# Score rows by VectorE's square transposes, and mask fills by ScalarE, in a four-layer graph attention kernel

## The chip, the cores and the metric

The kernel runs on one core of a Trainium2 chip. The metric is the device time of one launch in microseconds (us). A profile of one execution stands beside it; times inside it are read from that execution.

## The reference

128 small graphs of 128 nodes with 512 features each pass through four graph-attention layers. In every layer the features are normalised and rectified, the layer is applied, and its output is added to its input:

```python
for layer in (L0, L1, L2, L3):
    h = maximum(layernorm(x), 0)
    x = x + layer(h, adj)
```

Layer 1 has four heads of 256 columns and then a second attention with one head. Layer 3 has eight heads of 64 columns:

```python
# layer 1, first part (softmax over the source axis, per head)
xl = (x @ W1).reshape(B, N, H, F)
asrc, adst = einsum(xl, att_src), einsum(xl, att_dst)
e = leaky_relu(asrc[:, :, None, :] + adst[:, None, :, :], 0.2)
attn = softmax(where(mask, e, -1e9), axis=1)
# layer 3
xh = (x @ W_proj) by heads
scores = leaky_relu(a_src[..., None] + a_dst[..., None, :] + b_att, 0.2)
att = softmax(where(A > 0, scores, -1e30), axis=-1)
out = relu(att @ xh)
```

All arithmetic is in float32. A score is the sum of one number per row node and one number per column node. The number of the row node is a column of 128 values over the partitions, which an engine can add as a per-partition bias. The number of the column node is needed as a row of 128 values that is the same on every partition. Making such rows is what this case is about.

## The kernel before, in words

A graph is a generator (`graph`, with `layer0` to `layer3`) that yields one instruction, or a group of instructions, at a time. Ten graphs are in flight (`FLYING = 10`). A planner (`Scheduler`) merges their instructions into one program order ahead of time: at each step it issues the instruction that could start earliest by its own cost figures (`Step.estimate`), and the older graph where two are equal. The order on each engine is therefore fixed, and an engine that waits for one instruction holds up all that stand behind it. A stream that needs a buffer takes it (`Take`) from a named set of fixed size and stops until one is given back. PSUM has eight banks, all taken under the name `bank`.

The steps that the change touches:

- **Rows through HBM.** `rows_in_dram` takes some columns (4 for layer 1's `fx`, 16 for layer 3's `f`, 8 for layer 3's `mx`). TensorE transposes them against `ident` into a bank, ScalarE copies the bank to the tile `r`, one transfer on SyncE's queue (SP) writes `r` to a small HBM buffer `d`, and `d` is then read back with every partition receiving all of it.
- **Layer 1.** A second SP transfer spreads `d` over the score tile `e` (`e<-d`, 256 KB). VectorE then adds the mask and takes the maximum of each head.
- **Layer 3.** The tile `sd` holds the scores of eight heads in two arrangements, `d` and `e`, each 128x1024. First each half is filled with eight copies of a 128x128 mask (`m3`, and its transpose `m3t`) by an SP transfer of 512 KB from SBUF to SBUF. Then the rows of `f` are added to the whole of `sd` by an accumulating transfer that GpSimd (POOL) issues (`sd<-d`, 1024 KB). VectorE takes the maxima of `d`; they become `mx`, go through `rows_in_dram` again, and a second accumulating transfer (512 KB) subtracts them in `e`. ScalarE applies its Prelu head by head and one exponential, and TensorE multiplies (`x,sd`).
- **The last five graphs** (`LATE = 5`) build layer 3's rows on TensorE and VectorE instead (`add_rows`), without HBM.

Of the kernel before, what the change touches and what calls it, by code (L numbers as in the profile page):

```python
# [19 lines left out]
SLOPE = 0.2  # L20
EPS = 1e-5
FLYING = 10
AHEAD = 2
LATE = 5
# [18 lines left out]
class Step:  # L43
# [17 lines left out]
    def estimate(self, name, outs, ins, kw):  # L61

        if name == "dma_start":

            rate, busy = (290e3, 0.35) if self.engine == "SP" else (105e3, 1.0)
            self.moves = size(outs[0]) * outs[0].shape[0] * 4 / rate
            return busy, 1.0
        n = max(size(a) for a in outs[:1] + ins)
        if self.engine == "PE":
            if name == "transpose":  # L70
                return 0.109, 0.2
            return 2 * max(0.00084 * size(outs[0]), 0.108), 0.2
        if self.engine == "DVE":
            if name == "bn_stats":
                return 0.6, 0.12
            if name == "bn_aggr":
                return 0.09, 0.12
            per = 1 / 960
            if name == "tensor_scalar" and n >= 256:
                per /= 2  # L80
            return n * per + 0.07, 0.12
        if self.engine == "ACT":
            pointers = sum(isinstance(kw.get(k), bass.AP) for k in ("bias", "scale"))
            busy = n * 0.00081 + 0.105 + (0, 0.075, 0.135)[pointers]
            return busy + 0.1 * ("accum_out" in kw), 0.15
        if self.engine == "POOL":
            if kw.get("op") == ALU.pow or ALU.pow in kw.get("ops", ()):
                return 0.6, 0.1
            return (0.25 if n <= 16 else 0.55 if name == "tensor_scalar" else 1.3), 0.1
        raise ValueError(name)  # L90


class Group(Step):
    def __init__(self, steps):
        self.engine = steps[0].engine
        self.calls = [c for s in steps for c in s.calls]
# [3 lines left out]
        self.delay = steps[-1].delay  # L100


# [33 lines left out]
class Scheduler:  # L136
# [100 lines left out]
    def issue(self):  # L237
# [17 lines left out]
        if step.moves:  # L255

            self.moved = max(end, self.moved) + step.moves
            end = self.moved + 1.0
        for name in step.writes:
# [20 lines left out]
def kernel(  # L280
# [30 lines left out]
    K3 = l3_watt.shape[1] // 2  # L311
    AG = 4 if B % 4 == 0 else 1


# [128 lines left out]
    def fold(blocks, vecs, per, to):  # L443
# [4 lines left out]
        for g in range(0, len(blocks), 4):  # L448
            wt = yield from transposed(blocks[g : g + 4], "ht", 3)
            yield Group(  # L450
                [
                    T.matmul(
                        pf[:, j // per * k : (j // per + 1) * k],
                        lhsT=wt[:, j - g, :],
                        rhs=vecs[:, j, :],
                        start=(j % per == 0),
                        stop=(j % per == per - 1),
                    )
                    for j in range(g, g + 4)
                ]  # L460
            )
            give_back(wt)
        n = len(blocks) // per * k
# [32 lines left out]
    def norm_relu(xt):  # L496

        st6 = column("st6", nc.vector.BN_STATS_DIM)
        yield V.bn_stats(st6, xt)
        mv = column("mv", nc.vector.BN_AGGR_DIM)  # L500
        yield V.bn_aggr(mv, st6)
        ve = column("ve")
        yield G.tensor_scalar(ve, mv[:, 1:2], EPS, None, ALU.add)
        rstd = column("rstd")
        yield G.tensor_tensor(out=rstd, in0=ve, in1=minus_half, op=ALU.pow)
        nmr = column("nmr")
        yield V.scalar_tensor_tensor(nmr, mv[:, 0:1], -1.0, rstd, ALU.mult, ALU.mult)
        h = yield tile_of("h", 4, D)
        yield A.activation(out=h, in_=xt, func=AF.Relu, bias=nmr, scale=rstd)
        return h  # L510

# [17 lines left out]
    def transposed(blocks, tag, bufs):  # L529

        n = len(blocks)
        r = yield tile_of(tag, bufs, n, P)
# [4 lines left out]
        yield A.copy(r.rearrange("p m q -> p (m q)"), pt[:, : n * P])  # L537
        give_back(pt)
        return r

    def rows_in_dram(cols, n):

        r = yield Take(work, [2 * H3, P], "r", 4)
        r = r[:n]
        pt = yield bank()
        yield T.transpose(pt[:n, :P], cols, ident)
        yield A.copy(r, pt[:n, :P])
        give_back(pt)
        d = dram.tile([n, P], F32, tag=f"d{n}", name="d")
        yield S.dma_start(out=d, in_=r)  # L550
        give_back(r)
        return d.rearrange("n q -> (n q)").partition_broadcast(P)

    def spread(cols, n, to):

        d = yield from rows_in_dram(cols, n)
        yield S.dma_start(out=to, in_=d)

# [18 lines left out]
    def added(cols, to, late, rows=None):  # L577

        if late:
            yield from add_rows(cols, to)  # L580
            return
        if rows is None:
            rows = yield from rows_in_dram(cols, cols.shape[1])
        yield G.dma_start(out=to, in_=rows, accum_op=ALU.add)

    def attention(own, rows, e, mask, nh, exact=False):

        mx = column(f"mx{nh}", nh)  # L590
        yield Group(
            [
                V.tensor_tensor_reduce(
                    out=e[:, j, :],
                    in0=rows[j],
# [9 lines left out]
        )  # L605
        if rows[0].tensor.name != e.tensor.name:
            give_back(rows[0])
# [6 lines left out]
        if exact:  # L614
            ef = e.rearrange("p h q -> p (h q)")
            yield V.tensor_scalar(ef, ef, own, None, ALU.add)
            yield V.scalar_tensor_tensor(ef, ef, SLOPE, ef, ALU.mult, ALU.max)
        else:
            for j in range(nh):
                yield A.activation(  # L620
                    out=e[:, j, :],
                    in_=e[:, j, :],
                    func=AF.Prelu,
# [3 lines left out]
        for j in range(nh):  # L627
            yield A.activation(
                out=e[:, j, :],
                in_=e[:, j, :],  # L630
                func=AF.Exp,
# [7 lines left out]
    def attended(own, other, mask, values, exact=False):  # L639

        e = yield tile_of("e0", 3, 1, P)
        pb = yield bank()
        yield T.transpose(pb[:, :P], other.to_broadcast([P, P]), ident)
        rz = yield from attention(own, [pb[:, :P]], e, mask, 1, exact)
        et = yield from transposed([e[:, 0, :]], "et0", 3)
        give_back(e)
        pa = yield bank()
        yield T.matmul(pa, lhsT=et[:, 0, :], rhs=values, start=True, stop=True)
        give_back(et)
        return pa, rz  # L650

    def projected(lhs, n_k, w, parts, to, beside=None, plus=None):
# [4 lines left out]
        for i in range(parts):  # L657
            lo = i * width
            pm = yield bank()
            for g in range(0, n_k, 4):  # L660
# [3 lines left out]
                            pm[:, :width],  # L664
                            lhsT=lhs[:, c, :],
                            rhs=w[c][:, lo : lo + width],
# [40 lines left out]
    def layer1(xt, mask):  # L707
# [4 lines left out]
        fx = yield tile_of("xl", 2, E1 + HF)  # L712
        e = yield tile_of("e1", 3, H1, P)
        rows = e.rearrange("p h q -> p (h q)")
        fork = yield from projected(
            ht, KC, w1x, 3, columns(fx, 3), lambda: spread(fx[:, :H1], H1, rows)
        )
        give_back(ht)
        xl = fx[:, E1:]
        yield Join(fork)  # L720
        rz = yield from attention(fx[:, H1:E1], [e[:, j, :] for j in range(H1)], e, mask, H1)
        yield V.tensor_tensor(e, e, rz.unsqueeze(2).to_broadcast([P, H1, P]), ALU.mult)
        et = yield from transposed([e[:, j, :] for j in range(H1)], "et1", 3)
        give_back(e)
        y = yield tile_of("y1", 2, FC, P)
        for g in range(0, FC, 4):
# [5 lines left out]
                        lhsT=xl[:, c * P : (c + 1) * P],  # L732
                        rhs=et[:, c * P // F1, :],
                        start=True,
# [11 lines left out]
            give_back(po)  # L746
        give_back(fx, et)
        yf = y.rearrange("p c q -> p (c q)")
# [8 lines left out]

        yield from projected(y, FC, w2x, 2, columns(gx, 2), plus=columns(b2, 2))
        give_back(y)
# [17 lines left out]
    def layer3(xt, mask, mask_t, late):  # L777
# [22 lines left out]
        )  # L800
        give_back(ht)
        f = small.tile([P, 2, H3], F32, tag="f3", name="f3")
# [72 lines left out]
    def graph(b):  # L875
# [91 lines left out]
```

## Time and profile before

| | |
|---|---|
| median of 3 runs | 3410.86 us (3410.47 to 3410.93) |
| profiled execution, its own time | 3414.4 us |
| span of its trace | 3412.6 us |
| TensorE matmul busy | 3381.6 us, 99% of the span |
| VectorE busy | 2617.3 us, 77% |
| ScalarE busy | 2316.5 us, 68% |
| GpSimd busy | 871.6 us, 26% |
| moved by DMA | 450.33 MB, mean 132 GB/s |

The busy time of TensorE counts each matmul from its start to a modelled end, and neighbours overlap; what one costs in a full stream is the distance from its start to the next start. PE is TensorE's matmuls, PEld its weight loads, DVE VectorE, ACT ScalarE, POOL GpSimd, and SPq the queue on which SyncE issues transfers. Nearly all instructions have one line number, because the planner issues them; the names of the tiles tell them apart.

### The profile page before, as it was taken

The page shows a single profiled execution, that of the slowest core. Times are in us where ns is not written, and L with a number is a line of the kernel's source. Part 1 is how long each engine was busy: PE and PEld are TensorE (multiplying, and loading weights), DVE is VectorE, ACT ScalarE, POOL GpSimd, SP SyncE. Part 2 cuts the span into 40 slices and gives each one's busy share as a digit, 9 for nine tenths or more (in the row PEclk, how much of TensorE's full clock was granted, in tenths as well). Part 3 has the DMA queues.
Part 4 walks back from the last instruction along what each step waited for, and adds up shares of the span by engine and source line. Part 5 has one row for each costly group of instructions (what it writes and reads, how often), then busy time and mean ns, then how long its engine had stood idle before and what let it go on. Part 6 is the DMA issues. An engine that isn't in the chain of part 4 may idle for free.

```text
span 3412.6 us, 56516 instructions
## 1 busy us (share of the span) xinstructions
PE 3381.6 (99%) x17118; PEld 2650.2 (78%) x17118; DVE 2617.3 (77%) x9296; ACT 2316.5 (68%) x6661; POOL 871.6 (26%) x1791
## 2 busy tenths in 40 slices
PE   8999999999999999999999999999999999999998
PEld 5777777777777777777777777777777777777787
DVE  6777777777778777777777787777787777777766
ACT  4667676677677667666767766776776676667764
POOL 1222322222222222222222222222222222222221
PEclk7999999999999999999999999999999999999998
DMA  5155555555556556555655555565565555556553
GB/s 151 45 125 127 139 139 132 131 142 138 131 126 151 129 132 145 132 128 140 143 130 132 133 144 133 138 142 128 123 151 134 134 138 135 131 131 143 131 126 97
DMA packets 392879, 450.33 MB, mean 132 GB/s; under 512 B 27128, under 2 KB 309120, under 8 KB 376832
## 3 DMA queue, kind: packets, MB, share of 16 engines
q0 software_dynamic: 35424, 193.48, 29.3%
q1 hardware_dynamic: 352976, 253.23, 25.4%
q8 instruction: 137, 2.24, 0.3%
q14 instruction: 166, 1.36, 0.1%
q10 hardware_dynamic: 4176, 0.02, 0.1%
HBM read 277.11 MB, written 35.33 MB: 92 GB/s over the span
## 4 chain that ended last, share of the span: by engine, by line
PE 98%; ACT 1%; DVE 1%; issue 0%; DMA 0%; POOL 0%; ACTq 0%; POOLq 0%; DVEq 0%
PE bank L252 98%; DVE sd L252 0%; ACT ht L252 0%; DMA a<-in_L_gnn_a_dram 0%; ACT h L252 0%; ACT sd L252 0%; ACT e L252 0%; DMA at<-in_adj_dram 0%; POOL rstd L252 0%; DVE st L252 0%; DVE products L252 0%; DVE xt L252 0%; DVE e L252 0%; POOL ve L252 0%; DVE mx L252 0%
## 5 line engine op out<-in xcount | busy, mean ns | idle before, releaser
L252 PE MATMUL bank<-w2x,y 128*128 128x257 f32 x4096 | 975.2, 381 | 0.0
L252 PE MATMUL bank<-w1x,ht 128*128 128x344 f32 x3072 | 954.3, 454 | 1.4 <-ACT ht L252 1.4
L252 PEld LDWEIGHTS bank<-w2x,y 128*128 128x128 f32 x4096 | 746.8, 190 | 108.3 <-issue 16.7
L252 PEld LDWEIGHTS bank<-w1x,ht 128*128 128x128 f32 x3072 | 572.2, 191 | 261.1 <-issue 17.9
L252 ACT ACTIVATE h<-xt,nmr,rstd 128x512 f32<-128x512 f32 x512 | 413.6, 808 | 386.1 <-DVE nmr L252 385.0
L252 PE MATMUL bank<-wpx,ht 128*128 128x264 f32 x2048 | 501.9, 388 | 0.0
L252 POOL TENSOR_SCALAR ve<-mv 128x1 f32<-128x1 f32 x512 | 173.5, 339 | 1095.1 <-DVE mv L252 905.5
L252 PEld LDWEIGHTS bank<-wpx,ht 128*128 128x128 f32 x2048 | 381.1, 191 | 87.4 <-DVE y L252 8.6
L252 ACT ACTIVATE sd<-sd,f 128x128 f32<-128x128 f32 x1024 | 366.2, 392 | 0.0
L252 ACT ACTIVATE e<-e,nm 128x128 f32<-128x128 f32 x896 | 351.4, 396 | 13.8 <-DVE e L252 9.5
L252 DVE BATCH_NORM_STATS2 st<-xt 128x6 f32<-128x512 f32 x512 | 350.7, 685 | 0.0
L252 POOL TENSOR_TENSOR rstd<-ve,minus_half 128x1 f32<-128x1 f32 x512 | 313.7, 613 | 42.0
L252 PEld LDWEIGHTS bank<-x,sd 128*128 128x128 f32 x2048 | 266.1, 194 | 48.2 <-issue 12.2
L252 POOL DMA_DIRECT2D sd<-d x246 | 230.7, 994 | 267.5 <-ACT sd L252 136.7
L252 PEld LDWEIGHTS bank<-et,xl 128*128 128x128 f32 x2048 | 250.3, 192 | 38.4 <-issue 37.5
L252 PE MATMUL bank<-et,xl 128*128 128x128 f32 x2048 | 271.8, 276 | 0.2 <-ACT et L252 0.2
L252 PE MATMUL bank<-x,sd 128*128 128x65 f32 x2048 | 260.1, 271 | 7.2 <-ACT sd L252 7.2
L252 PE MATMUL bank<-h,et 128*128 128x512 f32 x512 | 266.1, 601 | 0.7 <-ACT et L252 0.7
L252 ACT COPY xl<-bank 128x344 f32<-128x344 f32 x384 | 166.7, 434 | 135.0 <-PE bank L252 134.6
L252 DVE TENSOR_TENSOR y<-bank,b 128x512 f32<-128x512 f32 x256 | 176.8, 690 | 81.4 <-PE bank L252 72.9
L252 ACT COPY x<-bank 128x264 f32<-128x264 f32 x256 | 96.0, 375 | 210.1 <-PE bank L252 209.9
L252 DVE SCALAR_TENSOR_TENSOR xt<-bank,rz,xt 128x512 f32<-128x512 f32 x256 | 191.3, 747 | 23.6 <-PE bank L252 23.5
(90 smaller groups left out, 5207.0 us busy)
## 6 DMA issues: line engine op xcount, KB each, us to landing
sd<-d POOLq DMA_DIRECT2D x123, 1024.0 KB, 11.0
sd<-m SPq DMA_DIRECT2D x128, 512.0 KB
sd<-m3t SPq DMA_DIRECT2D x128, 512.0 KB
sd<-d POOLq DMA_DIRECT2D x123, 512.0 KB, 8.3
xt<-in_x_dram SPq DMA_DIRECT2D x128, 256.0 KB
e<-d SPq DMA_DIRECT2D x128, 256.0 KB
out_dram<-xt SPq DMA_DIRECT2D x128, 256.0 KB
at<-in_adj_dram SPq DMA_DIRECT2D x32, 256.0 KB
```

What stands on the lines that cost most here:

```text
L252: method(*args, **kw)
```

## The change

`rows_in_dram` no longer uses TensorE, a bank or ScalarE. VectorE transposes 128x32 columns in squares of 32x32, so that a row of 128 values comes out as four pieces of 32 on four groups of partitions, and four SP transfers write the pieces to `d`. Where there are fewer than 32 columns they are repeated to fill the square (layer 3), or the next columns of the same tile come along unused (layer 1). Layer 3's two mask fills become two ScalarE copies of 128x1024. Besides, the planner's cost figures for transfers are other ones, one graph instead of two is loaded ahead, five small tiles of the normalisation become one (`st`, six buffers), and some buffer sets change: `r` 4 to 5 (of another shape), `et1` 3 to 2, `m1` 10 to 7.

```diff
-AHEAD = 2
+AHEAD = 1
@@ estimate
-            rate, busy = (290e3, 0.35) if self.engine == "SP" else (105e3, 1.0)
-            self.moves = size(outs[0]) * outs[0].shape[0] * 4 / rate
-            return busy, 1.0
+            moved = size(outs[0]) * outs[0].shape[0] * 4
+            if self.engine == "POOL":
+                self.moves = moved / 165e3
+                return 1.0, 3
+            run = 4 * min(a.shape[-1] for a in outs + ins)
+            self.moves = moved / (280e3 if run > 512 else 220e3)
+            return (0.5 if max(len(a.shape) for a in outs + ins) > 2 else 0.35), 1.5
@@ issue
-            end = self.moved + 1.0
+            end = self.moved + 0.3
@@ tile_four_gat_layers_kernel
+    Q = nc.vector.STREAM_SQUARE_SIZE
+    R = P // Q
@@
-    def rows_in_dram(cols, n):
-        r = yield Take(work, [2 * H3, P], "r", 4)
-        r = r[:n]
-        pt = yield bank()
-        yield T.transpose(pt[:n, :P], cols, ident)
-        yield A.copy(r, pt[:n, :P])
-        give_back(pt)
-        d = dram.tile([n, P], F32, tag=f"d{n}", name="d")
-        yield S.dma_start(out=d, in_=r)
+    def rows_in_dram(cols, n, heads_inside=False):
+        r = yield tile_of("r", 5, Q)
+        yield V.transpose(r, cols)
+        d = dram.tile([R, n, Q] if heads_inside else [n, R, Q], F32, tag=f"d{n}", name="d")
+        yield Group(
+            [
+                S.dma_start(
+                    out=d[c] if heads_inside else d[:, c], in_=r[c * Q : c * Q + n]
+                )
+                for c in range(R)
+            ]
+        )
         give_back(r)
-        return d.rearrange("n q -> (n q)").partition_broadcast(P)
+        return d.rearrange("n c b -> (n c b)").partition_broadcast(P)
+
+    def repeated(cols):
+        n = cols.shape[1]
+        return cols.unsqueeze(1).to_broadcast([P, Q // n, n])
@@ added
-            rows = yield from rows_in_dram(cols, cols.shape[1])
+            rows = yield from rows_in_dram(repeated(cols), cols.shape[1])
@@ layer1
-        fork = yield from projected(
-            ht, KC, w1x, 3, columns(fx, 3), lambda: spread(fx[:, :H1], H1, rows)
-        )
+        def rows():
+            d = yield from rows_in_dram(fx[:, :Q], H1)
+            yield S.dma_start(out=e, in_=d)
+        fork = yield from projected(ht, KC, w1x, 3, columns(fx, 3), rows)
...
-        et = yield from transposed([e[:, j, :] for j in range(H1)], "et1", 3)
+        et = yield from transposed(heads, "et1", 2)
@@ layer3
         for to, m in (d, mask), (e, mask_t):
-            yield S.dma_start(out=to, in_=m.unsqueeze(1).to_broadcast([P, H3, P]))
+            yield A.copy(to, m.unsqueeze(1).to_broadcast([P, H3, P]))
             give_back(m)
...
-        fork = None if late else (yield Fork(rows_in_dram(mx, H3)))
+        fork = None if late else (yield Fork(rows_in_dram(repeated(mx), H3)))
@@ graph
-        m1 = yield tile_of("m1", FLYING, P)
+        m1 = yield tile_of("m1", 7, P)
```

More of the change, by code (lines that the diff above doesn't have):

```diff
@@ L100, in __init__ @@
         self.delay = steps[-1].delay
+        self.moves = sum(s.moves for s in steps)
 class Take:
@@ L453, in fold @@
                         pf[:, j // per * k : (j // per + 1) * k],
-                        lhsT=wt[:, j - g, :],
+                        lhsT=wt[j - g],
                         rhs=vecs[:, j, :],
@@ L461, in fold @@
             )
-            give_back(wt)
+            give_back(wt[0])
         n = len(blocks) // per * k
@@ L496, in norm_relu @@
     def norm_relu(xt):
[L498 to L504, printed above, removed]
+        n = nc.vector.BN_STATS_DIM
+        st = yield tile_of("st", 6, n + 5)
+        yield V.bn_stats(st[:, :n], xt)
+        mean, var = st[:, n : n + 1], st[:, n + 1 : n + 2]
+        yield V.bn_aggr(st[:, n : n + 2], st[:, :n])
+        ve, rstd, nmr = (st[:, i : i + 1] for i in range(n + 2, n + 5))
+        yield G.tensor_scalar(ve, var, EPS, None, ALU.add)
         yield G.tensor_tensor(out=rstd, in0=ve, in1=minus_half, op=ALU.pow)
-        nmr = column("nmr")
-        yield V.scalar_tensor_tensor(nmr, mv[:, 0:1], -1.0, rstd, ALU.mult, ALU.mult)
+        yield V.scalar_tensor_tensor(nmr, mean, -1.0, rstd, ALU.mult, ALU.mult)
         h = yield tile_of("h", 4, D)
         yield A.activation(out=h, in_=xt, func=AF.Relu, bias=nmr, scale=rstd)
+        give_back(st)
         return h
@@ L531, in transposed @@
         n = len(blocks)
-        r = yield tile_of(tag, bufs, n, P)
+        r = yield tile_of(tag, bufs, n * P)
         pt = yield bank()
@@ L536, in transposed @@
         )
-        yield A.copy(r.rearrange("p m q -> p (m q)"), pt[:, : n * P])
+        yield A.copy(r, pt[:, : n * P])
         give_back(pt)
-        return r
-    def rows_in_dram(cols, n):
-        r = yield Take(work, [2 * H3, P], "r", 4)
-        r = r[:n]
-        pt = yield bank()
-        yield T.transpose(pt[:n, :P], cols, ident)
-        yield A.copy(r, pt[:n, :P])
-        give_back(pt)
-        d = dram.tile([n, P], F32, tag=f"d{n}", name="d")
-        yield S.dma_start(out=d, in_=r)
+        return blocks_of(r)
+    def rows_in_dram(cols, n, heads_inside=False):
[10 more added lines that the diff above has]
+        )
         give_back(r)
-        return d.rearrange("n q -> (n q)").partition_broadcast(P)
-    def spread(cols, n, to):
-        d = yield from rows_in_dram(cols, n)
-        yield S.dma_start(out=to, in_=d)
+        return d.rearrange("n c b -> (n c b)").partition_broadcast(P)
+    def repeated(cols):
+        n = cols.shape[1]
+        return cols.unsqueeze(1).to_broadcast([P, Q // n, n])
     def add_rows(cols, to):
@@ L582, in added, with attention @@
         if rows is None:
-            rows = yield from rows_in_dram(cols, cols.shape[1])
+            rows = yield from rows_in_dram(repeated(cols), cols.shape[1])
         yield G.dma_start(out=to, in_=rows, accum_op=ALU.add)
-    def attention(own, rows, e, mask, nh, exact=False):
+    def attention(own, rows, e, mask, exact=False):
+        nh = len(e)
         mx = column(f"mx{nh}", nh)
@@ L593, in attention @@
                 V.tensor_tensor_reduce(
-                    out=e[:, j, :],
+                    out=e[j],
                     in0=rows[j],
@@ L605, in attention @@
         )
-        if rows[0].tensor.name != e.tensor.name:
+        if rows[0].tensor.name != e[0].tensor.name:
             give_back(rows[0])
@@ L614, in attention @@
         if exact:
-            ef = e.rearrange("p h q -> p (h q)")
-            yield V.tensor_scalar(ef, ef, own, None, ALU.add)
-            yield V.scalar_tensor_tensor(ef, ef, SLOPE, ef, ALU.mult, ALU.max)
+            yield V.tensor_scalar(e[0], e[0], own, None, ALU.add)
+            yield V.scalar_tensor_tensor(e[0], e[0], SLOPE, e[0], ALU.mult, ALU.max)
         else:
@@ L620, in attention @@
                 yield A.activation(
-                    out=e[:, j, :],
-                    in_=e[:, j, :],
+                    out=e[j],
+                    in_=e[j],
                     func=AF.Prelu,
@@ L628, in attention @@
             yield A.activation(
-                out=e[:, j, :],
-                in_=e[:, j, :],
+                out=e[j],
+                in_=e[j],
                 func=AF.Exp,
@@ L639, in attended @@
     def attended(own, other, mask, values, exact=False):
-        e = yield tile_of("e0", 3, 1, P)
+        e = yield tile_of("e0", 3, P)
         pb = yield bank()
         yield T.transpose(pb[:, :P], other.to_broadcast([P, P]), ident)
-        rz = yield from attention(own, [pb[:, :P]], e, mask, 1, exact)
-        et = yield from transposed([e[:, 0, :]], "et0", 3)
+        rz = yield from attention(own, [pb[:, :P]], [e], mask, exact)
+        (et,) = yield from transposed([e], "et0", 3)
         give_back(e)
         pa = yield bank()
-        yield T.matmul(pa, lhsT=et[:, 0, :], rhs=values, start=True, stop=True)
+        yield T.matmul(pa, lhsT=et, rhs=values, start=True, stop=True)
         give_back(et)
@@ L664, in projected @@
                             pm[:, :width],
-                            lhsT=lhs[:, c, :],
+                            lhsT=lhs[c],
                             rhs=w[c][:, lo : lo + width],
@@ L712, in layer1 @@
         fx = yield tile_of("xl", 2, E1 + HF)
-        e = yield tile_of("e1", 3, H1, P)
-        rows = e.rearrange("p h q -> p (h q)")
-        fork = yield from projected(
-            ht, KC, w1x, 3, columns(fx, 3), lambda: spread(fx[:, :H1], H1, rows)
-        )
-        give_back(ht)
+        e = yield tile_of("e1", 3, H1 * P)
+        heads = blocks_of(e)
+        def rows():
+            d = yield from rows_in_dram(fx[:, :Q], H1)
+            yield S.dma_start(out=e, in_=d)
+        fork = yield from projected(ht, KC, w1x, 3, columns(fx, 3), rows)
+        give_back(ht[0])
         xl = fx[:, E1:]
         yield Join(fork)
-        rz = yield from attention(fx[:, H1:E1], [e[:, j, :] for j in range(H1)], e, mask, H1)
-        yield V.tensor_tensor(e, e, rz.unsqueeze(2).to_broadcast([P, H1, P]), ALU.mult)
-        et = yield from transposed([e[:, j, :] for j in range(H1)], "et1", 3)
+        rz = yield from attention(fx[:, H1:E1], heads, heads, mask)
+        e3 = e.rearrange("p (h q) -> p h q", h=H1)
+        yield V.tensor_tensor(e3, e3, rz.unsqueeze(2).to_broadcast([P, H1, P]), ALU.mult)
+        et = yield from transposed(heads, "et1", 2)
         give_back(e)
@@ L732, in layer1 @@
                         lhsT=xl[:, c * P : (c + 1) * P],
-                        rhs=et[:, c * P // F1, :],
+                        rhs=et[c * P // F1],
                         start=True,
@@ L746, in layer1 @@
             give_back(po)
-        give_back(fx, et)
+        give_back(fx, et[0])
         yf = y.rearrange("p c q -> p (c q)")
@@ L756, in layer1 @@
         gx = yield tile_of("x2", 2, E2 + D)
-        yield from projected(y, FC, w2x, 2, columns(gx, 2), plus=columns(b2, 2))
+        yl = [y[:, c] for c in range(FC)]
+        yield from projected(yl, FC, w2x, 2, columns(gx, 2), plus=columns(b2, 2))
         give_back(y)
@@ L800, in layer3 @@
         )
-        give_back(ht)
+        give_back(ht[0])
         f = small.tile([P, 2, H3], F32, tag="f3", name="f3")
```

## The prediction

> **What bounds the kernel now.** I read the page first: busy time of each engine (section 1) and the chain that ended last (section 4).
>
> ```profile
> PE 3381.6 (99%) x17118; PEld 2650.2 (78%) x17118; DVE 2617.3 (77%) x9296; ACT 2316.5 (68%) x6661; POOL 871.6 (26%) x1791
> ...
> PE 98%; ACT 1%; DVE 1%; issue 0%; DMA 0%; POOL 0%; ACTq 0%; POOLq 0%; DVEq 0%
> ```
>
> TensorE is busy all the time and is 98% of the chain. Whether it also streams without gaps, the view by stretches tells (window, length, then busy us and instructions of PE, PEld, DVE, ACT, POOL, clock, DMA share, GB/s), with the longest of PE's own waits (total, times, longest).
>
> ```profile
> 0.00:100.00 100.00, 84.47 (x325) 59.12 (x326) 69.74 (x247) 47.02 (x120) 13.54 (x35) 0.81 0.44 131
> ...
> 300.00:1700.00 1400.00, 1400.00 (x7126) 1099.23 (x7125) 1086.53 (x3887) 971.94 (x2804) 371.85 (x756) 1.00 0.57 136
> 1700.00:3300.00 1600.00, 1598.87 (x8131) 1254.90 (x8130) 1237.34 (x4407) 1106.00 (x3193) 418.44 (x858) 1.00 0.57 134
> ...
> 3350.00:3412.00 62.00, 49.38 (x286) 42.32 (x284) 40.43 (x102) 25.74 (x66) 5.02 (x18) 0.83 0.30 98
> ```
>
> ```profile
> PE bank L252 <- ACT sd L252: 7.2, 4, 2.9
> PE bank L252 <- ACT ht L252: 5.5, 9, 0.8
> ```
>
> From 100 to 3300 us PE is idle for about 1 us, at full clock. Waits lie only in the first 100 us and the last 60. So a microsecond taken off PE's stream comes off the time, as long as nobody else makes PE wait. Its price is not the busy time (0.27 us each) but the distance of starts, which the timeline of PE shows:
>
> ```profile
> 1508.82 0.27 PE L252 MATMUL bank<-ident,m 128*128 128x128 f32 x1
> 1508.93 0.27 PE L252 MATMUL bank<-ident,x 128*128 128x128 f32 x1
> 1509.04 1.90 PE L252 MATMUL bank<-w2x,y 128*128 128x257 f32 x8
> ...
> 1550.23 0.27 PE L252 MATMUL bank<-ident,xl 128*4 128x128 f32 x1
> 1550.34 1.02 PE L252 MATMUL bank<-h,et 128*128 128x512 f32 x2
> ```
>
> A transpose takes 0.11 us of the stream (0.109 on the mean of hundreds), also the one with four columns; the instruction before it is not made longer.
>
> **What the Trainium skill says.** Perfetto Trace Analysis (Identifying the Most-Contended Engine) calls matmul busy time no good measure, since matmuls are pipelined. The trace agrees: 0.27 busy, 0.11 apart. VectorE: DVE Perf Modes (The three transpose paths) says that VectorE transposes within 32x32 blocks only, into SBUF, and gives 311 ns for 128x128 in bf16; no run here shows one yet. ScalarE: Activation LUTs (What ACT_TABLE_LOAD costs) gives 186 ns + 0.833 ns per element for an activation with immediate operands, 1039 ns at 1024. The trace has 1047 ns for an exponential of that size. DMA: Bandwidth & Descriptors (Anatomy of one DMA) puts about 2 us of fixed time on each transfer; below, a small write is 2.66 us from issue to its reader's start.
>
> **The change, part by part.**
>
> 1. *TensorE.* Removed are the transposes in these groups:
>
> ```profile
> L252 PE MATMUL bank<-ident,xl 128*4 128x128 f32 x128 | 34.9, 272 | 0.0
> L252 PE MATMUL bank<-ident,f 128*16 128x128 f32 x123 | 33.5, 273 | 0.0
> L252 PE MATMUL bank<-ident,mx 128*8 128x128 f32 x123 | 33.5, 272 | 0.0
> ```
>
> 128 + 123 + 123 = 374; the changed program's TensorE order is shorter by just these. 374 x 0.109 = **40.8 us**, all on the path. Three banks fewer are taken per graph.
>
> 2. *ScalarE.* Gone are 374 copies to `r`: 32.2 + 30.3 + 30.2 = 92.7 us busy. New are 256 copies of 128x1024 at 1.05: 268 us. Net +175, to 2492 us, 74% of the new span. Hidden under PE, at nothing, while ScalarE still empties each bank in time.
>
> 3. *VectorE.* 374 transposes of 32 columns. At least the smallest VectorE instruction (`nmr<-mv,rstd`, 153 ns), at most the skill's 311 ns: 57 to 116 us. I take 0.17, near the other small ones: +64, to 2681 us, 80%. Hidden; at the high end 81%, still hidden.
>
> 4. *SP's queue.* Gone: the fills (0.60 and 0.67 us of issue, 163 us in all) and 374 row writes of 0.285. New: 1496 writes of about 0.285. Net +157 us, 1.2 us per graph; behind them stand `e<-d`, the output and the next `x`. A row is complete about 0.86 us later than with one write. SP spent 1862.9 us waiting for `r`, so it has room, and PE waits for nothing of it.
>
> 5. *DMA.* 134 MB of fills in 512-byte pieces go (256 x 512 KB), 30% of what is moved. PE never waited for them: nothing directly. But they ran beside the accumulating transfers, which should land sooner.
>
> 6. *The order.* The planner's costs and buffer sets differ, so the order differs everywhere. This is the one term that the counts do not give. I priced each TensorE order by the distances of starts in the trace (w1x 0.289, w2x 0.218, wpx 0.224, x,sd 0.105, transposes 0.109). The new order is strictly periodic, 25.7 us per graph. From the last wpx matmul of a graph to its x,sd it leaves 32.75 us where the old left 40.6. One graph of the trace shows what must fit:
>
> ```profile
> 1514.03 1.87 POOL L252 DMA_DIRECT2D sd<-d  x2 [1.89 <-DMA d<-r]
> 1527.88 1.19 DVE L252 TENSOR_REDUCE mx<-sd 128x8 f32<-128x1024 f32 x1
> 1534.99 0.27 PE L252 MATMUL bank<-ident,mx 128*8 128x128 f32 x1
> 1545.17 1.04 ACT L252 ACTIVATE sd<-sd 128x1024 f32<-128x1024 f32 x1
> 1549.39 1.00 PE L252 MATMUL bank<-x,sd 128*128 128x65 f32 x8
> ```
>
> ```profile
> sd<-d POOLq DMA_DIRECT2D x123, 1024.0 KB, 11.0
> sd<-d POOLq DMA_DIRECT2D x123, 512.0 KB, 8.3
> ```
>
> Its wpx ended at 1508.82 (first timeline), so it took 40.6 us. Of these, 3.2 lie between the exponential's end and x,sd, 4.7 between `mx` (ready at 1530.28) and its transpose in PE's queue, and about 2.9 between landing (1514.03 + 11.0) and the maximum: 29.8 are left. The change adds 2 x 0.86 on SP; each PE and ScalarE step on the way (about 0.8) becomes one of VectorE: some 31 us with the old landings. With less beside them (one 512 KB transfer alone early in the trace landed in 5.1) I estimate 25 to 28 (31 less some 3 us for each landing). It fits, so the new order costs PE nothing. The other gaps exceed what their steps need: rows of layer 1 to `e` transposes 37.1 us, where four issues, 2.66, a 256 KB read and some 6 us of scores need about 17; `et1` copied within 3.35, where the two fills and the copy need 2.7.
>
> *Sum.* 40.8 off the profiled execution: span 3412.6 to 3371.8, own time 3414.4 to 3373.6. The median of the runs lies 3.5 below that own time, so **3370 us**. Head and tail (about 35 and 20 us lost, by the starts) are ordered anew as well; I give them 8 us either way.
>
> **The rivals.**
>
> *A, slower: layer 3's shorter distance is too short.* POOL issues in order and ScalarE's exponential waits for the landing with all bank copies behind it. If the landings stay at 11.0 and 8.3 and the queues of VectorE and ScalarE, both fuller, add what they add today (10.8, less the 4.7 on PE), the chain is 37, not 32.75. PE then waits at x,sd in every graph; 1.28 graphs lie in that distance, so each us over costs 0.78 us per graph, 100 us in all. It decides from 0.4 us over (33.2). One us over: +100 - 41, about 3470. For it: 74% and 80% on in-order engines. Against it: the fills leave the DMA engines, and most of today's waiting is slack. 6%.
>
> *B, no change: the fills block ScalarE.* Two copies, 2.1 us, stand in the new order right ahead of the `et1` copy that the et,xl matmuls wait for. The margin is 3.35 - 2.7. If `e` transposes meet ScalarE later than ordered and PE waits 0.3 us per graph, 128 x 0.3 = 38 us go: 3408. PEld already waited for ScalarE's `e` 123 times, 34 us in all, without stopping PE, so margins are thin. Half of this (3389) is likelier than all. 8%, half of it still faster.
>
> *C, more: head and tail shrink too.* The way through layer 3 is 8 us shorter in the order and the first fills need no transfer. Up to 18 us: 3352. Against it: the tail ends in the five late graphs, which keep TensorE's transposes. 7%.
>
> *D: only transfers were hidden, nothing is gained.* Were the freed PE time eaten elsewhere, PE would show waits; the 374 are gone for certain, so this is B or A by another name and gets no chance of its own.
>
> **How the numbers follow.** Forecast 79% (3362 to 3379), C 7%, B 8%, A 6%. The range of 8 in 10 is the forecast with half of B and most of C: 3355 to 3389. A measurement here can tell 0.2%, 6.8 us, from no change: below 3404 is faster: 79 + 7 + 4 = 90%; 4% same; 6% slower.
>
> **What would show it.** Right: 16744 matmuls, PE without waits from 100 to the last 60 us, `sd<-m` copies near 1.05 us, transposes of `r` at 0.15 to 0.31, landings below 11.0 and 8.3, ScalarE near 74%. Wrong: PE waiting for `sd` some hundred times (A) or for `et` (B), or a mean distance of starts above 25.7 us per graph.

## The result, and the profile after

The changed kernel takes 3366.88 us (median of 4 runs, 3365.77 to 3370.39) against 3410.89 us for the kernel before on the same chip: a ratio of 0.9871, with a 95% interval of 0.9853 to 0.9888. A second set of runs gave 3369.06 us and 0.9880 (0.9866 to 0.9895). The profiled execution took 3365.79 us, with a span of 3364.0 us; that of before was 3412.6, so 48.6 us are to be accounted for. The medians lie 44.0 apart: the profiled execution of before was the slowest of its four (3414.34 us), that of after one of the two fastest.

The page of the kernel after: busy time of each engine, what the DMA engines moved, the shares of the chain that ended last, and the two accumulating transfers (KB each, median us from issue to landing).

```profile
PE 3330.1 (99%) x16744; PEld 2630.4 (78%) x16744; DVE 2642.4 (79%) x9670; ACT 2496.1 (74%) x6543; POOL 926.8 (28%) x1791
...
DMA packets 147431, 316.18 MB, mean 94 GB/s; under 512 B 47280, under 2 KB 63664, under 8 KB 131376
...
PE 98%; DVE 1%; ACT 1%; issue 0%; POOL 0%; DMA 0%; ACTq 0%
...
sd<-d POOLq DMA_DIRECT2D x123, 1024.0 KB, 8.0
sd<-d POOLq DMA_DIRECT2D x123, 512.0 KB, 5.0
```

TensorE is still the whole chain, now with 374 fewer instructions. The fills are gone from the DMA engines (450.33 to 316.18 MB), and the accumulating transfers land 3 us sooner. The stretches of after (length, then busy us and instructions of PE, PEld, DVE, ACT, POOL, clock, DMA share, GB/s):

```profile
0.00:100.00 100.00, 84.64 (x349) 60.07 (x350) 71.75 (x265) 48.95 (x125) 14.67 (x37) 0.86 0.44 130
...
300.00:1700.00 1400.00, 1400.00 (x7067) 1107.62 (x7066) 1113.01 (x4111) 1063.16 (x2791) 397.85 (x766) 1.00 0.44 97
1700.00:3250.00 1550.00, 1550.00 (x7814) 1226.43 (x7813) 1227.90 (x4514) 1173.16 (x3080) 439.99 (x847) 1.00 0.44 96
...
3300.00:3364.00 64.00, 45.49 (x253) 37.87 (x252) 37.48 (x99) 29.95 (x71) 4.50 (x14) 0.79 0.07 25
```

In the middle PE is busy 1400.00 of 1400 and 1550.00 of 1550 us. PE's own waits in after (total, times, longest) are those of the head and the tail, as before:

```profile
PE bank L256 <- ACT sd L256: 7.0, 4, 2.8
PE bank L256 <- ACT ht L256: 4.5, 8, 0.7
PE bank L256 <- ACT et L256: 1.1, 2, 0.6
```

The new instructions, by groups with their forms (total busy us, mean ns of one):

```profile
L256 ACT COPY sd<-m3t 128x1024 f32<-128x1024 f32 x128 | 133.5, 1043 | 0.0
L256 ACT COPY sd<-m 128x1024 f32<-128x1024 f32 x128 | 132.2, 1032 | 0.0
...
L256 DVE STREAM_TRANSPOSE r<-f 128x32 f32<-128x32 f32 x123 | 26.1, 212 | 22.1 <-POOL f L256 5.8
...
L256 DVE STREAM_TRANSPOSE r<-mx 128x32 f32<-128x32 f32 x123 | 25.4, 207 | 0.0
```

By the starts on PE, the 48.6 us are: 40.8 from 374 x 0.109; 5.1 from late starts behind `x,sd` (matmuls that begin later behind the one before than is usual for its form; 6.3 us in before and 1.2 in after, between 300 and 3200 us; an experiment below is about them), 1.3 from one stall of PE near 3022 us that after doesn't have; and 5.2 less lost in the head (the first 100 us), against 4.5 more lost in the tail (from 3200 us on). The sum is 47.9.

### The profile page after: what moved, and what is told of

It reads as the page before. It is cut to its first block, busy times and chain, and to the rows that moved or that the text cites. A ratio compares the mean times of both kernels' runs of the same rounds, so it can differ in the third digit from the quotient of the medians.

```text
span 3364.0 us, 57116 instructions
## 1 busy us (share of the span) xinstructions
PE 3330.1 (99%) x16744; PEld 2630.4 (78%) x16744; DVE 2642.4 (79%) x9670; ACT 2496.1 (74%) x6543; POOL 926.8 (28%) x1791
## 2 busy tenths in 40 slices
DMA packets 147431, 316.18 MB, mean 94 GB/s; under 512 B 47280, under 2 KB 63664, under 8 KB 131376
## 4 chain that ended last, share of the span: by engine, by line
PE 98%; DVE 1%; ACT 1%; issue 0%; POOL 0%; DMA 0%; ACTq 0%
PE bank L256 98%; DVE sd L256 0%; DVE products L256 0%; ACT e L256 0%; ACT ht L256 0%; ACT sd L256 0%; DVE st L256 0%; POOL st L256 0%; DMA a<-in_L_gnn_a_dram 0%; DVE mx L256 0%; DVE t L256 0%; DVE e L256 0%; DVE xt L256 0%; ACT h L256 0%; DVE rz L256 0%
## 5 line engine op out<-in xcount | busy, mean ns | idle before, releaser
L256 ACT ACTIVATE h<-xt,st 128x512 f32<-128x512 f32 x512 | 414.8, 810 | 168.4 <-DVE st L256 166.5
L256 POOL TENSOR_SCALAR st<-st 128x1 f32<-128x1 f32 x512 | 225.6, 441 | 848.7 <-DVE st L256 435.7
L256 POOL TENSOR_SCALAR m<-m 128x128 f32<-128x128 f32 x128 | 71.9, 562 | 1117.7 <-DVE st L256 1056.9
L256 POOL TENSOR_TENSOR st<-st,minus_half 128x1 f32<-128x1 f32 x512 | 334.6, 654 | 42.3
L256 ACT ACTIVATE sd<-sd,f 128x128 f32<-128x128 f32 x1024 | 326.0, 387 | 0.0
L256 PEld LDWEIGHTS bank<-et,xl 128*128 128x128 f32 x2048 | 259.6, 192 | 61.5 <-issue 31.4
L256 DVE RECIPROCAL rz<-z 128x1 f32<-128x1 f32 (+1 forms) x512 | 83.6, 163 | 270.1 <-ACT e L256 266.6
```

What stands on the lines that cost most here:

```text
L256: method(*args, **kw)
```

## The experiments

The theory was that the transposes taken off TensorE are the whole gain. The rivals were that the fills by ScalarE cost something (B), that layer 3's shorter way is near its edge (A), and that the new order itself gives or takes time. Each run is set against the kernel before, run beside it on the same chip.

**Rows alone** (`x1_rows`). The kernel before with the new `rows_in_dram` and nothing else: fills by SP, the old cost figures.

```diff
-        pt = yield bank()
-        yield T.transpose(pt[:n, :P], cols, ident)
-        yield A.copy(r, pt[:n, :P])
...
+        r = yield tile_of("r", 5, Q)
+        yield V.transpose(r, cols)
...
```

> The kernel before with the row part alone: square transposes and four writes; the mask fills stay SP transfers and the planner keeps its costs. Theory (PE's stream is what counts; 374 transposes at 0.109 us): 3411 - 41 = 3370, 3366 to 3376; landings of the accumulating transfers stay near 11.0 and 8.3 us; PE without waits in the middle. Rival 1 (the gain is the fills leaving the DMA engines): 3405 to 3413. Rival 2 (the gain needs the new order): PE waits in the middle, 3380 to 3411.

3370.14 us (3368.81 to 3372.38), ratio 0.9881 (0.9868 to 0.9895), with 16744 matmuls and no wait of PE in the middle. Within the intervals the row part alone gives the whole gain. One thing went otherwise than expected: the accumulating transfers land after 9.5 and 5.4 us, not near 11.0 and 8.3, though the fills are all there.

**Fills alone** (`x2_fills`). The kernel before with the two fills copied by ScalarE.

```diff
-            yield S.dma_start(out=to, in_=m.unsqueeze(1).to_broadcast([P, H3, P]))
+            yield A.copy(to, m.unsqueeze(1).to_broadcast([P, H3, P]))
```

> The kernel before with the mask fills alone moved to ScalarE. Theory: hidden on both sides, 3411 within 4 us; landings fall from 11.0 and 8.3 to about 8 and 5; ScalarE at 2316 + 266 = 2583 us, 76%. Rival 1 (the fills are the gain): 3367 to 3400. Rival 3 (two fills in front of bank copies block ScalarE): slower, up to 3450, PE waiting for et or e.

3423.3 us (3417.72 to 3425.2), ratio 1.0033 (1.002 to 1.0046): slightly slower, where I had expected nothing. PE doesn't wait in the middle, so ScalarE isn't the reason. The profiled execution has a span 5.8 us longer than before: 6 us of late starts behind `x,sd` (223 instead of 113, taken up below) and 7 more lost in the tail, against 6 less in the head and 1.3 for the stall of before. The medians lie 13 us apart; what the other runs lost is not shown.

**The fills back on SP, the rest as after** (`x5_dmafills`): the diff above reversed, in the kernel after.

> The changed kernel with the mask fills back on SP as transfers of 512 KB. Theory: 3367 within 5 us, since PE's stream has the same matmuls and the planner leaves 37.9 us from wpx to x,sd; landings again 10 to 11 and 8. Rival 1 (the fills are the gain): 3380 to 3411.

3444.62 us (3442.98 to 3444.97), ratio 1.0098 (1.0084 to 1.0112): 78 us slower than after, and a clear miss. The landings are not to blame (8.3 and 5.3 us). The waits of x5, over all engines:

```profile
POOL sd L256 <- ACT e L256: 568.1, 117, 6.8
ACT e L256 <- DVE st L256: 162.2, 117, 3.3
DVE r L256 <- POOL f L256: 117.9, 117, 2.9
...
PE bank L256 <- ACT et L256: 33.3, 118, 2.2
```

Four waits happen 117 or 118 times, once per graph. The timeline of x5 puts them in order (start us, length, engine, in brackets the idle time before and its releaser):

```profile
1518.86 0.94 POOL L256 DMA_DIRECT2D sd<-d  x1 [4.87 <-ACT e L256]
...
1520.72 0.21 POOL L256 TENSOR_TENSOR f<-x,b_l 128x16 f32<-128x16 f32 x1
1520.97 0.21 DVE L256 STREAM_TRANSPOSE r<-f 128x32 f32<-128x32 f32 x1 [0.97 <-POOL f L256]
1521.58 0.40 ACT L256 ACTIVATE e<-e,nm 128x128 f32<-128x128 f32 x1 [1.34 <-DVE st L256]
...
1524.19 1.12 PE L256 MATMUL bank<-x,et 128*128 128x512 f32 x2 [0.23 <-ACT et L256]
```

GpSimd stands 4.87 us at an accumulating transfer of one graph, the second, which by the program needs ScalarE's eight Prelus of that graph's scores. The sum `f` of another graph is queued behind it, with two short instructions of a normalisation between. VectorE's new transpose `r<-f` waits for that `f`, with VectorE's other work behind it; ScalarE waits for VectorE, and so `et` of layer 1's second attention is late for TensorE. In this order TensorE had left 1.74 us between the transpose of `e0` and `x,et` at that place; the order of after has 4.02 there. Summed by the starts, PE lost 0.44 us in each of 113 graphs ahead of `x,et` (50 us), 12 between the two `x,et` that follow such a stop, and 12 in late starts behind `x,sd`.

**`f` on VectorE** (`x10_f_on_dve`): x5 with one instruction moved, so that the supposed chain is cut at one link.

```diff
-        yield G.tensor_tensor(f, fx[:, :, :E3].rearrange("p h s -> p s h"), b_l3, ALU.add)
+        yield V.tensor_tensor(f, fx[:, :, :E3].rearrange("p h s -> p s h"), b_l3, ALU.add)
```

> x5_dmafills with one instruction on another engine: f, the sum of layer 3's score columns and their bias, is made by VectorE and not by GpSimd, so that it doesn't stand behind the accumulating transfer that waits for ScalarE's e. The order on TensorE leaves the same distances as x5's at every step (1.74 us from the e0 transpose of layer 1's second attention to its x,et). Theory: VectorE's wait for f behind GpSimd made et late; without it PE doesn't stop in the middle: 3370 (3362 to 3385), no 100 waits of PE for et, and of VectorE for f of GpSimd none. Rival: the 1.74 us alone are too short, whatever GpSimd does: 3445, with PE waiting for et in more than 100 graphs as before. In between: GpSimd's other work (rstd, m2) behind the same transfer keeps half of it, 3400 to 3425.

3387.19 us (3386.76 to 3388.0), ratio 0.9934 (0.9918 to 0.9951): 57 us faster than x5, 2 us beyond the expected range. The waits of x10:

```profile
POOL sd L256 <- ACT e L256: 567.5, 117, 6.8
...
PE bank L256 <- ACT et L256: 3.4, 3, 1.2
```

GpSimd waits as long as before, and nobody on the path stands behind it any more: PE's 118 waits for `et` are 3. TensorE's order is that of x5 for its first 16,311 of 16,744 matmuls, so the 1.74 us are long enough when VectorE doesn't wait for `f`. That chain was 57 of the 78 us that x5 lost. What x10 still has over after is 11 us of late starts behind `x,sd`, some 7 in the head and the tail, and two stops of PE.

**Each fill twice** (`x4_twofills`): after, with `A.copy(to, ...)` of both fills repeated; 256 copies more on ScalarE.

> The changed kernel with each mask fill done twice: 256 more ScalarE copies of 1.04 us, +266 us, ScalarE at about 2762 us, 82%. Theory (ScalarE has room, the order knows of it): 3367 within 5 us. Rival 3 (fills block the bank copies): PE waits for et, 0.3 us or more per graph, 3405 or more.

3373.25 us (3371.16 to 3373.53), ratio 0.989 (0.9875 to 0.9905), 1 us beyond the range. ScalarE rises to 2712.0 us, 80%, and PE has no wait in the middle; the 6 us over after are again late starts behind `x,sd` (114 places). Rival B falls: twice the suspected cost doesn't stop PE.

**The transposes put back, unread** (`x6_dummy`): after, with `T.transpose(pt[:, :P], ident, ident)` into a bank of its own in `rows_in_dram`, and nothing that reads it.

> The changed kernel with a 128x128 TensorE transpose of the identity into a bank that nobody reads put beside each square transpose: 374 transposes back, without their ScalarE copies. Theory (0.109 us of PE's stream each): 3367 + 41 = 3408 within 5 us. Rival (a lone transpose hides beside a neighbour's weight load, and the gain came from elsewhere): under 3385.

3414.31 us (3411.78 to 3417.54), ratio 1.0013 (1.0006 to 1.002), 1 us beyond the range. PE's timeline of x6 at one of the added transposes (`bank<-ident`):

```profile
1500.83 1.94 PE L256 MATMUL bank<-wpx,ht 128*128 128x264 f32 x8
1502.61 0.27 PE L256 MATMUL bank<-ident 128*128 128x128 f32 x1
1502.72 2.48 PE L256 MATMUL bank<-w1x,ht 128*128 128x344 f32 x8
```

From its start to the next start it is 109 ns on the mean (109 to 110 between 300 and 3200 us), and its neighbours take what they take elsewhere within 2 ns. The span is 3413.0, 49 us over after: 374 x 0.109 = 40.8 for the transposes, about 6 us of late starts (112 places) and 2 us in three stops. That is the price of the sum, measured by itself; ScalarE's copies were not put back, so they are not the gain.

**The old cost figures** (`x3_oldcosts`): after, with the planner's transfer costs of before (`rate, busy = (290e3, 0.35) if self.engine == "SP" else (105e3, 1.0)`, and delays of 1.0 us).

> The changed kernel with the planner's former transfer costs (290 and 105 KB per us, 1 us delays); it orders 38.5 us from wpx to x,sd instead of 32.75. Theory (the order only has to leave room): 3367 within 6 us. Rival 2 (the new costs are part of the gain): 3375 to 3411.

3375.69 us (3374.93 to 3377.1), ratio 0.9901 (0.9886 to 0.9915): outside my 3367 within 6, and inside the rival's range. PE stops in the middle only twice, 1.3 us in all, and 226 late starts behind `x,sd` (12 us) stand against none in after. The new figures are worth some 9 us, in this set of orders, and not because the old ones leave too little room.

**Layer 3's distance cut** (`x7_soon`): after, with a planner that believes the accumulating transfers to be fast.

```diff
-                self.moves = moved / 165e3
-                return 1.0, 3
+                self.moves = moved / 600e3
+                return 1.0, 0.3
```

> The changed kernel with a planner that believes accumulating transfers land far sooner (600 KB per us, 0.3 us delay); it orders only 27.9 us from wpx to x,sd. In the changed kernel's trace that chain needs 26.8 us without its queueing and took 32.7 with it. Theory: it just fits or PE starts to wait for sd; each us over costs 100 us in all: 3367 to 3470, and every us above 3367 shows as PE waiting for ACT sd in most graphs. Rival (the distance is of no account): 3367 within 3 us, no waits.

4435.13 us (4426.78 to 4448.27), ratio 1.3015 (1.2987 to 1.3044): some 965 us beyond even the upper end of the forecast. The order leaves 27.9 us from the last wpx matmul to x,sd, where after takes 32.7 with 5.9 of queueing in it. The waits of x7:

```profile
POOL sd L256 <- DMA d<-r: 687.5, 120, 8.0
DVE mx L256 <- DMA sd<-d: 601.1, 123, 9.8
ACT sd L256 <- DMA sd<-d: 540.8, 123, 6.5
PE bank L256 <- DVE r L256: 473.2, 116, 5.4
...
PE bank L256 <- ACT et L256: 189.1, 125, 4.2
```

The landings are what they were (8.3 and 5.2 us). What costs is that GpSimd, VectorE and ScalarE each stand still for this one graph in turn, in order, with the other graphs' work behind them. The longest of PE's stops, in the timeline of x7:

```profile
1497.81 1.22 DVE L256 TENSOR_REDUCE mx<-sd 128x8 f32<-128x1024 f32 x1 [6.06 <-DMA sd<-d]
...
1499.41 0.21 ACT L256 ACTIVATE mx<-mx 128x8 f32<-128x8 f32 x1 [5.86 <-DVE mx L256]
...
1499.82 0.24 ACT L256 COPY et<-bank 128x128 f32<-128x128 f32 x1
1499.86 0.21 DVE L256 STREAM_TRANSPOSE r<-mx 128x32 f32<-128x32 f32 x1
1500.11 2.08 PE L256 MATMUL bank<-x,et 128*128 128x512 f32 x2 [5.35 <-DVE r L256]
```

TensorE reads no `r`. All 116 waits put down to `r` stand before an `x,et`, and each of these starts 54 ns after ScalarE's copy of `et` has ended; the transpose `r<-mx` only ends at the same time. So it is `et` of another graph that TensorE lacks. The stops cost more than their length. The stretch behind this stop and the one after it (the clock is the third number from the end):

```profile
1499.00:1504.00 5.00, 3.89 (x6) 1.72 (x7) 4.69 (x25) 4.26 (x15) 1.40 (x3) 0.50 0.01 2
1505.00:1532.00 27.00, 23.57 (x122) 18.88 (x121) 14.04 (x48) 14.08 (x35) 5.41 (x11) 1.00 0.42 88
```

In each graph of the middle the granted clock is 0.50 for a stretch of mostly 6.8 us, and there the starts of two `h,et` lie 0.85 us apart instead of 0.43. PE waits 736 us in all (29 in after); matmuls that take longer than in after add some 310 of the 1066 us by which the spans differ. A graph takes 34.2 us instead of 25.6.

**What stands behind `x,sd`** (`x11_between`). The traces of all these kernels show one pattern. Where the first matmul behind a half of `x,sd` is a transpose, its successor starts on time within 10 ns; where it is a matmul of another form, its successor starts 52 to 56 ns late. In after all 227 halves between 300 and 3200 us are followed by a transpose, in before 109 of 222. The test is x10 with an unread transpose behind each half, in the same bank:

```diff
                     for k in range(i * half, (i + 1) * half)
                 ]
+                + [T.transpose(pa[:, 3 * P :], ident, ident)]
```

> x10_f_on_dve with one unread transpose of ident set on TensorE right behind each half of x,sd (256 in all, into the unused columns of the same bank). In every trace so far the first matmul after an x,sd half holds up its successor by 54 to 55 ns where it is a 128x128 to 128x512 matmul of another form (226 times in x10, 12 us), and by 0 to 9 ns where it is a transpose. Theory: what stands behind x,sd decides, so the 55 ns go here as well: late starts after x,sd 0, and the stream is longer by 256 x 0.109 - 12 = 16 us: 3403 (3396 to 3412). Rival: the 55 ns belong to those matmuls, wherever they stand in this order: 28 us longer, 3415, with the late starts one place further on. The order on TensorE leaves only 1.06 us at one place in half of the graphs (e0 transpose of layer 0 to its h,et), so PE may stop there; then the distances of starts behind x,sd still tell the two apart.

3407.15 us (3403.11 to 3412.55), ratio 0.9995 (0.9986 to 1.0004). PE's timeline of x10:

```profile
1504.99 1.00 PE L256 MATMUL bank<-x,sd 128*128 128x65 f32 x8
1505.83 1.94 PE L256 MATMUL bank<-h,et 128*128 128x512 f32 x4
1507.60 2.48 PE L256 MATMUL bank<-w1x,ht 128*128 128x344 f32 x8
```

and of x11:

```profile
1509.34 1.00 PE L256 MATMUL bank<-x,sd 128*128 128x65 f32 x8
1510.18 0.28 PE L256 MATMUL bank<-ident 128*128 128x128 f32 x1
1510.29 1.88 PE L256 MATMUL bank<-h,et 128*128 128x512 f32 x4
1512.01 1.32 PE L256 MATMUL bank<-w1x,ht 128*128 128x344 f32 x4
```

The same four `h,et` take 1507.60 - 1505.83 = 1.77 us of the stream in x10 and 1512.01 - 1510.29 = 1.72 in x11. At every one of x11's halves in the middle the 55 ns are gone: the transpose takes 113 to 119 ns where others take 109, and what follows is within 3 ns of its form. So the neighbour decides, and the rival, that the 55 ns belong to those matmuls, falls. As a cure it loses, since a transpose costs more than 55 ns; it pays only where the order has one to put there, as that of after does. Why it is so was not settled. One more figure belongs to it: in the same traces the first of the eight `x,sd` is followed by the second after 55 to 60 ns, where the others lie 109 to 112 apart. About as much as is gained there is lost behind the group; whether the two are one thing was not tested.

**More rows off TensorE** (`x8_morerows`, `x9_middle`). The single rows of layer 0, of layer 1's second attention and of layer 2 go the same way: in all graphs (x8), or in graphs 9 to 118 alone (x9). In both, the tile `e0` has four buffers instead of three.

```diff
-            pb = yield bank()
-            yield T.transpose(pb[:, :P], other.to_broadcast([P, P]), ident)
...
+            yield V.transpose(r, repeated(other))
...
+            yield S.dma_start(out=d, in_=r[::Q])
...
+            yield S.dma_start(out=e, in_=d.rearrange("c b -> (c b)").partition_broadcast(P))
```

> The changed kernel with the three single rows of a graph (layer 0, layer 1's second attention, layer 2) made the same way: a square transpose, one write of 512 bytes, a read of 64 KB to all partitions, in place of 384 TensorE transposes into a bank. Theory (PE's stream is what counts): 3367 - 384 x 0.109 = 3325, 3320 to 3332, if ten graphs in flight hide some 5 us more in each of three chains. Rival (those chains get too long, or SP's in-order queue does): PE waits, 3340 to 3450.

> The changed kernel, in which the single rows of layer 0, of layer 1's second attention and of layer 2 too go through VectorE's transpose, one strided write and a spread read, but for the middle 110 graphs only (9 to 118); the first and the last nine keep TensorE's transposes. Theory: TensorE is still the bound in the middle, and what x8 lost was the head alone, where a row through HBM takes some 5 us and no other graph is far enough on to fill the gap. 330 fewer transposes x 0.109 = 36 us off 3367, so 3331 (3323 to 3340), 16414 matmuls, the first 100 us as in the changed kernel. Rival: the loss of x8's head is moved to the place where the first graphs with the longer way start, or the fuller queues (SP, VectorE) make PE wait in the middle: 3345 to 3370.

> The changed kernel once more, on the same chip as x9_middle, so that the two can be set against each other: 3366 to 3370.

x8 took 3358.56 us (3355.05 to 3360.31), ratio 0.9849 (0.9834 to 0.9863); x9 took 3358.54 (3357.78 to 3362.48), 0.9852 (0.9837 to 0.9867), beside 3369.06 (3367.46 to 3370.37) for after on its chip. Both are some 0.3% better than after, and both missed their forecasts. In x8 the stream is shorter as worked out, by 42 us, but PE is busy 66.66 of the first 100 us where after has 84.64. In x9 the head is kept, and the loss comes where the way changes. The stretches of x9:

```profile
100.00:200.00 100.00, 98.14 (x472) 75.00 (x472) 64.36 (x246) 61.37 (x165) 21.74 (x42) 1.00 0.21 44
200.00:300.00 100.00, 94.58 (x467) 73.61 (x466) 82.68 (x306) 73.74 (x197) 29.10 (x56) 1.00 0.44 97
```

In the kernel after, PE is busy 100.00 us in each of these two. By the starts, and set against the second set of runs of after, x9 loses 11.8 us between 100 and 400 us, 7.9 in the middle (5 of them late starts), 6.5 more in the tail and 0.9 in the head, against 36.0 gained: 8.9 us are left, and the spans differ by 8.8. That is the rival named ahead of the run. x9 is the best of these kernels within the uncertainty, with x8.

## Why the prediction was right

The forecast was 3370 us (3355 to 3389), and the time is 3367 to 3369. The main term and what lies under it held: TensorE's stream is the time, and x1 and x6 show its price from both sides. For the profiled executions the sum was 7.8 us short (48.6 against 40.8), most of it in the order. That the median fits within 3 us is in part luck: before's profiled execution, from which the sum starts, was its slowest, and head and tail nearly cancelled. By its own steps:

1. *TensorE, 40.8 us.* Right: 16744 matmuls, and x6 measures the 374 at 0.109 us each.
2. *ScalarE, 2492 us and 74%, hidden.* 2496.1 and 74%; copies of 1.032 and 1.043 us against 1.05 taken. x4 shows that it stays hidden at 80%.
3. *VectorE.* Transposes of 0.205 to 0.212 us against the 0.17 I took, inside the range of 0.15 to 0.31. Its sum was over by 39 us all the same (2642.4 against 2681). The lengths of VectorE's instructions, added up, rose by 67.9 us (3171.4 to 3239.3), about the 64 of the forecast; but the records overlap, busy time counts an overlap once, and it rose by only 25. x4 has the very VectorE instructions of after and is at 2561.6. So lengths of single instructions can't be added to an engine's busy time. Hidden either way.
4. *SP's queue and DMA.* No wait of PE came from them. The landings fell to 8.0 and 5.0, as estimated (3 us each), but the fills are not shown to be the reason, so that the size came out is luck: x2, without fills, has 10.0 and 5.2, and with all fills x1 has 9.5 and 5.4 and x5 8.3 and 5.3.
5. *The order costs PE nothing.* It costs nothing, and the term was still mis-sized: it gives 6.4 us, 5.1 in late starts and 1.3 in a stall. The distances I priced with were means of each form, and the 55 ns depend on the pair. x10 and x11 show that; nothing in the list of counts would.
6. *Layer 3's chain, 25 to 28 us.* One graph of after, in its timeline:

```profile
1507.22 0.21 POOL L256 TENSOR_TENSOR f<-x,b_l 128x16 f32<-128x16 f32 x1 [2.89 <-ACT x L256]
1507.47 0.21 DVE L256 STREAM_TRANSPOSE r<-f 128x32 f32<-128x32 f32 x1
...
1512.39 0.96 POOL L256 DMA_DIRECT2D sd<-d  x1 [0.84 <-DMA d<-r]
...
1522.13 1.20 DVE L256 TENSOR_REDUCE mx<-sd 128x8 f32<-128x1024 f32 x1
...
1528.96 0.95 POOL L256 DMA_DIRECT2D sd<-d  x1
...
1536.88 1.04 ACT L256 ACTIVATE sd<-sd 128x1024 f32<-128x1024 f32 x1
...
1539.25 1.00 PE L256 MATMUL bank<-x,sd 128*128 128x65 f32 x8
```

Its wpx ended near 1506.5, so 32.7 us pass. Queueing is 1.7 between the landing (1512.39 + 8.0) and the maximum, 2.9 between the second landing (1528.96 + 5.0) and the exponential (1536.88), and 1.3 between the exponential's end and x,sd: 26.8 are needed.

7. *Head and tail, 8 us either way.* 5.2 us less lost in the head, 4.5 more in the tail. The last step of the sum, 3.5 us down from the profiled execution to the median, did not carry over to after, whose profiled execution lies 1.1 us below its median.

Rival A's mechanism is real, but its place and price were wrong. I had PE waiting at x,sd and 0.78 us per graph for each us that is short. In x7 the order is about 5 us short of what after takes, which would be 4 us per graph; measured are 8.6. PE waited for `et` of other graphs, since three in-order engines had stood still before it, and then ran at half the granted clock for a while. Rival B fell with x4. What I had missed as a risk is the one new wait that the change brings, VectorE behind GpSimd's `f`: 5.8 us in after, and 57 us for the kernel in x5's order. I had checked that each step's distance was long enough by itself, not who stands in whose queue.

## What to carry to other kernels

Where one engine is busy without gaps, count what leaves its stream and price it by the distance of starts; all else is worth only what it keeps from making that engine wait. When work is moved to an engine that takes orders in sequence, ask for each new wait what stands behind it and who needs that: one small sum queued behind a waiting transfer cost 57 us in x5. Undo the parts of a change one at a time and look at the order each time: x1 and x5 do nearly the same work and lie 74 us apart, and x7 has the very instructions of after.

## What the runs showed of the hardware

- The matmul that follows eight `x,sd` multiplications (128x65 each) delays its successor by 52 to 56 ns (some 1,600 times over ten traces), unless it is a transpose (0 to 10 ns). An inserted transpose takes the delay away (x11). The first of the eight is followed after 55 to 60 ns, the others after 109 to 112.
- The landing of the accumulating transfer of 1 MB didn't go with the bytes of the fills: 11.0 us with them in before, 9.5 in x1 and 8.3 in x5 and x10; 10.0 without them in x2 and 8.0 in after. What stands beside it in each order wasn't taken apart.
- VectorE's transpose of 128x32 in float32 takes 205 to 212 ns, whether its input is 32 columns of a tile or 8 or 16 columns repeated.
- In x7, where TensorE stops in each graph, for up to 5.4 us, the granted clock is 0.50 for a stretch of mostly 6.8 us in each graph, and 0.898 on the mean, against 0.992 in after. In the middle of before, where PE stops once for 1.1 us, it stays at 1.00.
